# Routed rows scaled where they are made, one scatter a turn, and the shared expert's chunks moved

## The chip, the cores and the metric

The kernel runs on one core of a Trainium2 chip. The time is that of one execution on the device, in microseconds, as the median of several runs; a profiled execution gives the trace. PE (matmuls), DVE (vector), ACT (scalar), POOL (GpSimd) and SP (which issues most DMAs) are the core's engines; each works through its own list of instructions in order, and semaphores tie the lists together.

## What is computed

A decoder layer on x of 2 x 1024 tokens with 256 columns, in float32: x plus a linear attention of layernorm(x), plus a cross-attention to 154 keys with 16 heads, plus a mixture of experts. The part that the change touches is the last:

```python
scores = softmax(xf @ gate_w.T)                 # 2048 tokens, 8 experts
_, idx = top_k(scores + gate_b, 2)
w = take_along_axis(scores, idx)                # the two scores of a token
h = silu((xf @ w1[e] + b1[e]) * (xf @ w3[e] + b3[e]))      # 352 hidden
y = sum over the token's two experts e of  w_e * (h @ w2[e] + b2[e])
z = the same expert formula with the shared weights, for every token
x = x + y + z
```

The 8 experts work only on the tokens that chose them; a token's two rows are found by routing.

## The kernel before

The 2048 tokens are four blocks of 512, each of four tiles of 128 tokens. The linear attention and norms come first; the cross-attention is one software-pipelined loop of 64 turns (one turn is a tile and four heads), `for n in range(N + 6)`. In turn n, PE computes the scores of turn n+1 (L1142), DVE weighs and masks them (L1151, L1163), ACT takes the exponential (L1172), POOL divides by the sums (`divide`, s at L1180 and sr at L1183, one turn later), and PE transposes the divided rows (L1096, in `turn`) three turns later and multiplies them by the values (L1114, L1123). Steps of other work (`ahead`) are drawn into the turns from a list: the layernorm of a finished block (`finish`, with rstd on POOL at L274 and L275 and xn on DVE at L280) and its `router`.

`router` takes a block's tokens: the scores (gate matmuls L790), the two choices, and for each token and choice the slot of a row in the table `x_tab` in DRAM. A row of `x_tab` holds the normalised token (256 columns), its number and a half code: DX = 258 columns. `scatter` (POOL: a small memset L871, then an indirect DMA L872) writes the 128 rows of a tile to the slots of one choice, so there are two scatters a tile, eight a block and 32 in all. They are appended to a list, `scatters`; `put_rows()` issues all that stand in it, once a turn (in the loop right after `divide`) and between the pieces of the list behind the loop. `router` appends two at a step. The scores that the chosen slots carry are gathered in `gate` (L885, L886).

Behind the loop a list written out by hand orders the rest: the last blocks' layernorm and router (`late`), the output projections (`wo`), the pieces of the shared expert (`dense[blk]`) and the table of routed blocks (`table`). A piece of `dense` is a chunk (one of three column groups of the hidden layer, eight matmuls L935, ACT L940, DVE L943, Silu L924) or two output tiles (L955, added to x by DVE at L961, for blocks 2 and 3 followed by the store L913).

Then `routed` works through 36 blocks of 128 slots, three stages deep: `fetch` (POOL gathers rows of `x_tab`, L1427), `turn_in` (transposes L1450, ACT copy L1454), `up` (L1462, DVE L1468 and L1472), `gate_up` (ACT Silu L1476), `turn_hidden` (L1482, DVE L1486 and the target row `to`, L1488 to L1494) and `down` (L1500, ACT copy to y L1508, POOL scatter to `y_tab` L1509). The first gathers wait for the last scatter of `x_tab`. At i == n of its loop, in the drain, it draws one piece of `dense[2]`; `weigh_rows`, drawn in at i == 4, sorts each token's two scores into the order of its two rows (`by`). A further body, for more than 36 blocks, runs only if the routing needs it; with these inputs it does not.

At the end `combine` loads the two rows of every token from `y_tab` (L1543, 16 loads of 256 KB on SP's queue) and adds them to x, each times its column of `by`, with one DVE scalar_tensor_tensor (L1550) for a tile and a choice: 32 of 128x256. Its steps alternate with the last pieces of `dense[2]` and `dense[3]`.

Of the kernel before, what the change touches and what calls it, by code (L numbers as in the profile page):

```python
# [15 lines left out]
P = 128  # L16
# [9 lines left out]
def tile_decoder_layer(  # L26
# [139 lines left out]

    DX = D + 2
    x_tab = tc.dram_tile([E * REG, DX], F32, name="x_tab")  # L170
    y_tab = tc.dram_tile([2 * NTOK + P, D], F32, name="y_tab")

# [612 lines left out]
    def router(part, blk, lnT, xn, t0, nt):  # L785
# [57 lines left out]
        nc.vector.tensor_tensor(eq, ch_t, row(halves), ALU.mult)  # L843
        nc.vector.tensor_reduce(xn[:, some, D + 1], eq, AX.X, ALU.add)
        nc.gpsimd.tensor_copy(xn[:, some, D], tok2[:, ts])
        yield
        pp = mm_tile()
        nc.tensor.matmul(
# [32 lines left out]
        for t in tiles:  # L881
            for i in range(2):
                scatters.append(lambda t=t, i=i: scatter(t, i))
            if t == t0:
                nc.vector.tensor_tensor(eq2, hot[:, :, ts, :], both(sc), ALU.mult)  # L885
                nc.vector.tensor_reduce(gate[:, :, ts], eq2, AX.X, ALU.add)  # L886
            yield

    puts = []
# [6 lines left out]

    gap_t = rwp.tile([P, 1], F32, tag="gap", name="gap_t")
    NT = NTOK // P
    gate = rwp.tile([P, 2, NT], F32, tag="gate", name="gate")
    slot = rwp.tile([P, 2, NT], I32, tag="slot", name="slot")  # L900
    carry = [rwp.tile([P, E], F32, tag=f"carry{i}", name=f"carry{i}") for i in range(NBLK + 2)]

# [140 lines left out]
    with bctx:  # L1043
# [257 lines left out]
        with region:  # L1301
            for pair in range(2):
                groups[0].q_proj(pair)()
            sc[0] = score(*steps[0])
            for n in range(N + 6):
                i, t = divmod(n, TPB)
                if n + 1 < N:
                    sc[n + 1] = score(*steps[n + 1])
                if n < N:
                    s = ss[n % len(ss)]  # L1310
                    weigh(*steps[n], sc.pop(n), s)
                for take in behind:
                    take()
                behind = []
                for take in later:
                    take()
                later.clear()
                if n < N:
                    nm = hide(*steps[n], s)
                take_later()  # L1320
                if 0 <= n - 3 < N:
                    g3, t3 = steps[n - 3]
                    g3.turn(t3, ss[(n - 3) % len(ss)], srs[(n - 3) % len(srs)])

                if n + LEAD < N:
                    g4, t4 = steps[n + LEAD]
                    g4.load(t4)
                if t < 2 and i + 1 < len(groups):
                    groups[i + 1].q_proj(t)()
                if open_ and (t % 2 == 0 or open_[0][0] == NBLK - 2):  # L1330
                    blk, u = open_.pop(0)
                    behind.append(project_out(blk, u))
                    if u == TPB - 1:
                        behind.append(lambda blk=blk: side.append(finish(blk)))
                if t == 3 and 0 < i <= len(groups):
                    gv = groups[i - 1]
                    take = gv.values()
                    take(0)
                    behind.append(lambda take=take: take(1))
                    if gv.g == NG - 1:  # L1340
                        open_ += [(gv.blk, u) for u in range(TPB)]
                ahead()
                if n == N - TPB:
                    hb = ctx.enter_context(tc.tile_pool(name="hb", bufs=2, side="right"))
                    Ws_sb = shared_weights(hb)
                    dense = [
                        shared_expert(blk, hb, Ws_sb, store if blk >= 2 else None)
                        for blk in range(NBLK)
                    ]
                if N <= n < N + NHC:  # L1350
                    on(dense[0], 1)
                elif n >= N:
                    ahead()


                if n < N:
                    sums[n] = power(s, nm)
                if n - 1 in sums:
                    divide(ss[(n - 1) % len(ss)], srs[(n - 1) % len(srs)], sums.pop(n - 1))
                if n < N:  # L1360
                    put_rows()
            for take in behind:
                take()
            while side:
                ahead()

            def project_out_of(blk, u):
                project_out(blk, u)()
                yield

            turns[0] = 0
            late = [finish(NBLK - 1), finish(NBLK)]
            wo = (None for of in open_ for _ in project_out_of(*of))
            put_rows(6)
            on(wo, 1)
            on(late[0], 1)
            tabs = ctx.enter_context(tc.tile_pool(name="tabs", bufs=1, side="right"))
            table = block_table(tabs)  # L1380
            next(table)
            for which, pieces in (
                (late[0], 1), (wo, 1), (late[0], 2), (wo, 1),
                (late[0], 1), (late[1], 1), (late[0], 1), (late[1], 1), (late[0], 3),
                (dense[1], 1), (late[1], 2), (dense[1], 1), (late[1], 1), (late[0], 1),
                (late[1], 2), (late[0], 2), (late[1], 2), (dense[1], 1), (dense[0], 1),
                (late[1], 1), (late[0], 1), (late[1], 1), (table, 1), (late[1], 2),
                (dense[0], 1), (dense[1], 2), (dense[2], 1),
            ):
                on(which, pieces)  # L1390
                put_rows()
# [26 lines left out]
    class Slots:  # L1418
# [59 lines left out]
        def turn_hidden(self):  # L1478
            i = self.i
            tp = mm_tile()  # L1480
            for c in range(NHC):
# [4 lines left out]
            nc.vector.tensor_copy(self.hT.rearrange("p c q -> p (c q)"), tp[:, :HW_])  # L1486
            to_f = mpool.tile([P, 1], F32, tag="to_f", name="to_f")
            nc.vector.scalar_tensor_tensor(  # L1488
                to_f, self.xb[:, D + 1 :], eidx[:, i : i + 1], self.xb[:, D : D + 1],
                ALU.is_lt, ALU.add,  # L1490
            )
            nc.vector.tensor_tensor(to_f, to_f, beyond[:, i : i + 1], ALU.add)
            self.to = mpool.tile([P, 1], I32, tag="to", name="to")
            nc.vector.tensor_tensor(self.to, to_f, away, ALU.min)  # L1494

        def down(self):
            po = mm_tile()
# [7 lines left out]
                    start=(c == 0), stop=(c == NHC - 1),  # L1505
                )
            y = mpool.tile([P, D], F32, tag="y", name="y", bufs=2)
            nc.scalar.copy(y, po[:, :D])  # L1508
            nc.gpsimd.indirect_dma_start(  # L1509
                out=y_tab, in_=y, in_offset=None,  # L1510
                out_offset=bass.IndirectOffsetOnAxis(ap=self.to[:, 0:1], axis=0),
            )


    by = tab_tile([P, 2, NT], "by")

    def weigh_rows():
        num = tab_tile([P, 2, NT, E], "num")
        nc.vector.tensor_tensor(
            num, hot,  # L1520
            iota_f[:, :E].unsqueeze(1).unsqueeze(1).to_broadcast([P, 2, NT, E]), ALU.mult,
        )
        who = tab_tile([P, 2, NT], "who")
        nc.vector.tensor_reduce(who, num, AX.X, ALU.add)
        swap = tab_tile([P, 2, NT], "swap")
        nc.vector.tensor_tensor(swap[:, 0], who[:, 0], who[:, 1], ALU.is_gt)
        nc.vector.tensor_scalar(swap[:, 1], swap[:, 0], -1.0, 1.0, ALU.mult, ALU.add)
        other = tab_tile([P, NT], "other")
        for i in range(2):
            nc.vector.tensor_tensor(by[:, i], gate[:, 0], swap[:, 1 - i], ALU.mult)  # L1530
            nc.vector.tensor_tensor(other, gate[:, 1], swap[:, i], ALU.mult)
            nc.vector.tensor_tensor(by[:, i], by[:, i], other, ALU.add)

    def combine():

        tiles = [(blk, t) for blk in (2, 3, 0, 1) for t in range(TPB)]
        yts = {}
        for blk, t in tiles:
            at = blk * TPB + t
            yt = yts[blk, t] = W_sb[:, at // 2, (at % 2) * 2 * D : (at % 2 + 1) * 2 * D].rearrange(  # L1540
                "p (i d) -> p i d", i=2
            )
            nc.sync.dma_start(  # L1543
                out=yt,
                in_=y_tab[2 * P * at : 2 * P * (at + 1), :].rearrange("(p i) d -> p i d", i=2),
            )
        for blk, t in tiles:
            at = blk * TPB + t
            for i in range(2):
                nc.vector.scalar_tensor_tensor(  # L1550
                    xr[blk][:, t, :], yts[blk, t][:, i, :], by[:, i, at : at + 1],
                    xr[blk][:, t, :], ALU.mult, ALU.add,
                )
            if blk < 2:
                store(blk, t)
            yield

    back = combine()
# [5 lines left out]
    def routed(blocks, fill=None):  # L1564
# [7 lines left out]
        for i in range(n + 2):  # L1572
# [7 lines left out]
                blocks[i + 2].turn_in()  # L1580
            if i < n:
                blocks[i].gate_up()
            elif fill and i == n:
                next(fill)
            if i >= 2:
                blocks[i - 2].down()
            if fill and i == 4:
                weigh_rows()


    NF = NB - (E - 1) // 2
# [2 lines left out]
        skip_runtime_bounds_check_because="a sum of counts of blocks",  # L1594
    )
    with tc.manual_schedule(engines=ENGINES):
        routed([Slots(i) for i in range(NF)], dense[2])
    with tc.If(used > NF):
        with tc.manual_schedule(engines=ENGINES):
            routed([Slots(i) for i in range(NF, NB)])  # L1600
    with tc.manual_schedule(engines=ENGINES):

        for blk, some in zip((2, 3, 3, 2, 3, 2, 3, 3), (1, 3, 3, 2, 3, 2, 2, 0)):
            next(dense[blk])
            on(back, some)

# [64 lines left out]
```

## Time and profile before

| what | value |
|---|---|
| median of 3 runs | 642.95 us (641.51 to 643.62) |
| profiled execution | 642.6 us, span 640.9 us |
| mean granted TensorE clock | 0.989 |
| PE busy | 602.3 us, 94% of the span |
| DVE busy | 432.5 us, 67% |
| ACT busy | 296.7 us, 46% |
| POOL busy | 249.3 us, 39% |
| cross-attention turns of the scatters of blocks 0 and 1 | 285 to 325 us, 360 to 384 us |
| routed blocks | 453 to 604 us |
| combine | 615 to 638 us |

The span is the time from the first to the last instruction in the trace; what lies outside it is 1.7 us. A line of a trace answer gives the start, the duration, the engine, the line of the kernel, the operation, the tiles written and read with their partitions and elements, and in brackets how long the engine had been idle and what ended that. Busy shares overlap between engines; what counts is which engine the others wait for in a stretch.

### The profile page before, as it was taken

Reading aid. Unit: us, or ns where it says so; the run is one execution under the profiler, and the core shown is the slowest. Engines: PE = TensorE matmul, PEld = TensorE weight load, DVE = VectorE, ACT = ScalarE, POOL = GpSimd, SP = SyncE. Lnnn points to the kernel's source line nnn. Section 1 sums busy time; section 2 is a strip of 40 time slices with the busy share of each in tenths; the row PEclk is TensorE's granted clock in tenths of the full one; section 3 lists DMA queues with packets and bytes.
Section 4 is the critical chain, followed back from the end, with each engine's and each line's share of the span. In section 5 each row is a group of like instructions: output and inputs, shape, how many; then the busy total and the mean of one; then the engine's idle time right before and its main releaser. Section 6 shows DMA issues by size and latency. Waiting matters only on the chain.

```text
span 640.9 us, 10242 instructions
## 1 busy us (share of the span) xinstructions
PE 602.3 (94%) x3024; PEld 389.2 (61%) x3024; DVE 432.5 (67%) x1380; ACT 296.7 (46%) x895; POOL 249.3 (39%) x377
## 2 busy tenths in 40 slices
PE   4998989999999998999999979999799999999996
PEld 3553556545677445776468554766577777777654
DVE  4877995789835899556975693367365665556547
ACT  2423586777636676446884665231222222222220
POOL 4913042522315223228642581625344444444110
PEclk9999999999999999999999989999899999999999
DMA  8800579967966554245552320798112122221065
GB/s 292 241 16 6 129 185 259 216 153 175 237 158 145 145 137 104 52 125 129 119 125 65 91 75 1 222 333 301 49 59 67 58 67 63 63 67 59 33 209 203
DMA packets 111683, 83.79 MB, mean 131 GB/s; under 512 B 41874, under 2 KB 105091, under 8 KB 111500
## 3 DMA queue, kind: packets, MB, share of 16 engines
q1 hardware_dynamic: 106588, 69.42, 42.1%
q0 software_dynamic: 4992, 13.71, 6.7%
q8 instruction: 26, 0.43, 0.3%
q14 instruction: 29, 0.24, 0.1%
q10 hardware_dynamic: 48, 0.00, 0.0%
HBM read 54.90 MB, written 27.98 MB: 129 GB/s over the span
## 4 chain that ended last, share of the span: by engine, by line
PE 64%; DVE 15%; POOL 6%; issue 4%; ACT 4%; DMA 3%; SPq 2%; DVEq 0%; POOLq 0%; ACTq 0%
PE sc L1462 14%; PE mm L1193 8%; PE mm L1500 6%; PE sc L935 5%; PE mm L1076 4%; PE mm L586 3%; PE sc L1142 3%; PE tp L1096 3%; DVE s L1163 3%; PE mm L1114 3%; POOL x_tab L872 3%; DVE rks L521 2%; DVE s L1151 2%; PE mm L494 2%; PE tp L1500 2%
## 5 line engine op out<-in xcount | busy, mean ns | idle before, releaser
L1180 POOL TENSOR_TENSOR s<-s,sums 128x512 f32<-128x512 f32 x64 | 66.8, 1044 | 179.6 <-DVE sums L1179 167.1
L1172 ACT ACTIVATE s<-s,nm 128x154 f32<-128x154 f32 x256 | 104.8, 417 | 5.7 <-DVE nm L1163 5.7
L1462 PE MATMUL sc<-W_sb,xT 128*128 x288 | 92.8, 466 | 0.2 <-issue 0.2
L1163 DVE CUSTOM_DVE_ANT_0 s<-s,mk 128x154 f32<-128x154 f32 x256 | 90.7, 408 | 1.2
L1509 POOL DMA_INDIRECT y_tab<-y,to x36 | 35.5, 985 | 83.6 <-DVE to_f L1488 57.4
L1462 PEld LDWEIGHTS sc<-W_sb,xT 128*128 128x128 f32 x288 | 52.8, 193 | 24.0 <-issue 1.7
L1468 DVE TENSOR_TENSOR ea<-sc,b 128x704 f32<-128x704 f32 x36 | 32.1, 892 | 51.9 <-PE sc L1462 51.8
L1076 PE MATMUL mm<-lnT,Wq_sb 128*128 128x512 f32 x128 | 61.6, 604 | 2.6 <-DVE k L516 2.0
L1097 ACT COPY pT<-tp 128x512 f32<-128x512 f32 x64 | 36.9, 576 | 45.1 <-PE tp L1096 44.8
L1193 PE MATMUL mm<-Wo_sb,oT 128*128 128x256 f32 x256 | 57.6, 379 | 0.0
L1142 PEld LDWEIGHTS sc<-kT,qT 64*128 64x128 f32 x512 | 36.5, 186 | 29.0 <-issue 10.9
L1142 PE MATMUL sc<-kT,qT 64*128 64x154 f32 x512 | 50.5, 316 | 3.5 <-DVE s L1151 2.8
L1193 PEld LDWEIGHTS mm<-Wo_sb,oT 128*128 128x128 f32 x256 | 48.0, 190 | 8.8 <-issue 2.4
L1151 DVE TENSOR_TENSOR s<-sc,fs 128x616 f32<-128x616 f32 x64 | 49.9, 780 | 0.9 <-PE sc L1142 0.9
L1096 PE MATMUL tp<-ident,s 128*128 128x128 f32 x256 | 42.7, 290 | 8.0 <-POOL s L1180 7.5
L1172 ACT ACTIVATION_READ_ACCUMULATOR s<-s,nm 128x1 f32 x256 | 49.6, 194 | 0.0
L935 PE MATMUL sc<-lnT,Ws_sb 128*128 128x512 f32 (+1 forms) x96 | 43.1, 595 | 0.8 <-ACT y L1508 0.4
L494 PE MATMUL mm<-lnT,wqkv_sb 128*128 128x512 f32 x88 | 41.4, 600 | 0.7 <-DVE lnT L225 0.4
L1500 PE MATMUL mm<-W_sb,hT 128*128 x168 | 41.1, 380 | 0.7 <-DVE to_f L1488 0.7
L1427 POOL DMA_INDIRECT xb<-x_tab,rows_i x36 | 34.7, 965 | 16.3 <-issue 9.4
L1096 PEld LDWEIGHTS tp<-ident,s 128*128 128x128 f32 x256 | 27.8, 144 | 20.1 <-issue 9.6
L872 POOL DMA_INDIRECT x_tab<-xn,slot x32 | 32.9, 1029 | 14.6 <-DVE req L885 9.6
(245 smaller groups left out, 1024.3 us busy)
## 6 DMA issues: line engine op xcount, KB each, us to landing
fs<-in_fside SPq DMA_DIRECT2D x64, 308.0 KB
x_tab<-book SPq DMA_DIRECT2D x32, 516.0 KB
W_sb<-in_w SPq DMA_DIRECT2D x16, 352.0 KB
mk<-in_mask SPq DMA_DIRECT2D x64, 77.0 KB
W_sb<-y_tab SPq DMA_DIRECT2D x16, 256.0 KB
b<-b_tab SPq DMA_DIRECT2D x1, 2816.0 KB
W_sb<-in_w SPq DMA_DIRECT2D x8, 256.0 KB
out<-xr SPq DMA_DIRECT2D x16, 128.0 KB
```

Of the source, the lines that this page charges most:

```text
L494: nc.tensor.matmul(ps, lhsT=wqkv_sb[:, c, o * P : (o + 1) * P], rhs=lnTa[self.blk][:, c, :], start=(c == 0), stop=(c == ND - 1),)
L935: nc.tensor.matmul(ps[:hn, :], lhsT=Ws_sb[:, at : at + hn], rhs=lnT[:, d, :], start=(d == 0), stop=(d == ND - 1),)
L1076: nc.tensor.matmul(ps, lhsT=Wq_sb[:, c, o * P : (o + 1) * P], rhs=lnTq[self.blk][:, c, :], start=(c == 0), stop=(c == ND - 1),)
L1096: nc.tensor.transpose(tp[:, j * P : (j + 1) * P], s[:, j, :P], ident)
L1142: nc.tensor.matmul(sc[:, par, pair * SK : (pair + 1) * SK], lhsT=gr.qT[pair][rows, t * P : (t + 1) * P], rhs=kT[rows, 2 * gr.g + pair, gr. ...
L1151: begun = nc.vector.tensor_tensor(s[:, :, :SK].rearrange("p (pair par) k -> p par pair k", par=2), sc[:, :, : 2 * SK].rearrange("p par (pa ...
L1163: nc.vector.tensor_tensor_reduce(s[:, j, :], s[:, j, :], gr.mk[t][:, j, :], MASKED, FLOOR, ALU.add, ALU.min, nm[:, j : j + 1],)
L1172: nc.scalar.activation(s[:, j, :SK], s[:, j, :SK], AF.Exp, bias=nm[:, j : j + 1], scale=-1.0, accum_out=sums[:, j : j + 1],)
L1180: nc.gpsimd.tensor_tensor(s[:, :, :P], s[:, :, :P], sums.unsqueeze(2).to_broadcast([P, HG, P]), ALU.mult)
L1193: nc.tensor.matmul(ps[:, :D], lhsT=oTs[blk][o][:, t * P : (t + 1) * P], rhs=Wo_sb[0][:, o, :], start=(o == 0), stop=(o == NO - 1),)
L1462: nc.tensor.matmul(ab[:, j, :HID], lhsT=self.xT[:, d, :], rhs=W_sb[:, bass.ds(ev, 1), at : at + HID].rearrange("p a h -> p (a h)"), start= ...
L1500: nc.tensor.matmul(po[:, :D], lhsT=self.hT[:kn, c, :], rhs=W_sb[:kn, bass.ds(self.ev, 1), O2 + c * D : O2 + (c + 1) * D].rearrange("p a d ...
```

## The change

Six edits:

1. A row of `x_tab` grows by eight columns and carries the token's eight scores (a POOL copy in `router`). The score gathers for `gate`, and `weigh_rows`, go.
2. In `turn_hidden` DVE copies the score of the block's expert out of the row (`by`, 128x1, at a register offset), and in `down` ACT scales y by it instead of copying.
3. `combine` then adds without a factor, and takes two tiles at once: 16 tensor_tensor of 128x512 instead of 32 of 128x256. The loads and stores are the same ones.
4. In the loop `put_rows(1)`: one scatter a turn.
5. Two chunks of `dense[2]` instead of one stand at the end of the list ahead of the gathers.
6. In the drain a piece is drawn at i == n and at i == n + 1 (the last chunk of `dense[2]`, the first of `dense[3]`); after it two chunks and eight output tiles are left instead of four and eight.

```diff
@@ -166,7 +166,7 @@
 
 
 
-    DX = D + 2
+    DX = D + 2 + E
     x_tab = tc.dram_tile([E * REG, DX], F32, name="x_tab")
     y_tab = tc.dram_tile([2 * NTOK + P, D], F32, name="y_tab")
 
@@ -843,6 +843,7 @@
         nc.vector.tensor_tensor(eq, ch_t, row(halves), ALU.mult)
         nc.vector.tensor_reduce(xn[:, some, D + 1], eq, AX.X, ALU.add)
         nc.gpsimd.tensor_copy(xn[:, some, D], tok2[:, ts])
+        nc.gpsimd.tensor_copy(xn[:, some, D + 2 :], sc)
         yield
         pp = mm_tile()
         nc.tensor.matmul(
@@ -881,9 +882,6 @@
         for t in tiles:
             for i in range(2):
                 scatters.append(lambda t=t, i=i: scatter(t, i))
-            if t == t0:
-                nc.vector.tensor_tensor(eq2, hot[:, :, ts, :], both(sc), ALU.mult)
-                nc.vector.tensor_reduce(gate[:, :, ts], eq2, AX.X, ALU.add)
             yield
 
     puts = []
@@ -896,7 +894,6 @@
 
     gap_t = rwp.tile([P, 1], F32, tag="gap", name="gap_t")
     NT = NTOK // P
-    gate = rwp.tile([P, 2, NT], F32, tag="gate", name="gate")
     slot = rwp.tile([P, 2, NT], I32, tag="slot", name="slot")
     carry = [rwp.tile([P, E], F32, tag=f"carry{i}", name=f"carry{i}") for i in range(NBLK + 2)]
 
@@ -1358,7 +1355,7 @@
                 if n - 1 in sums:
                     divide(ss[(n - 1) % len(ss)], srs[(n - 1) % len(srs)], sums.pop(n - 1))
                 if n < N:
-                    put_rows()
+                    put_rows(1)
             for take in behind:
                 take()
             while side:
@@ -1385,7 +1382,7 @@
                 (dense[1], 1), (late[1], 2), (dense[1], 1), (late[1], 1), (late[0], 1),
                 (late[1], 2), (late[0], 2), (late[1], 2), (dense[1], 1), (dense[0], 1),
                 (late[1], 1), (late[0], 1), (late[1], 1), (table, 1), (late[1], 2),
-                (dense[0], 1), (dense[1], 2), (dense[2], 1),
+                (dense[0], 1), (dense[1], 2), (dense[2], 2),
             ):
                 on(which, pieces)
                 put_rows()
@@ -1486,12 +1483,14 @@
             nc.vector.tensor_copy(self.hT.rearrange("p c q -> p (c q)"), tp[:, :HW_])
             to_f = mpool.tile([P, 1], F32, tag="to_f", name="to_f")
             nc.vector.scalar_tensor_tensor(
-                to_f, self.xb[:, D + 1 :], eidx[:, i : i + 1], self.xb[:, D : D + 1],
+                to_f, self.xb[:, D + 1 : D + 2], eidx[:, i : i + 1], self.xb[:, D : D + 1],
                 ALU.is_lt, ALU.add,
             )
             nc.vector.tensor_tensor(to_f, to_f, beyond[:, i : i + 1], ALU.add)
             self.to = mpool.tile([P, 1], I32, tag="to", name="to")
             nc.vector.tensor_tensor(self.to, to_f, away, ALU.min)
+            self.by = mpool.tile([P, 1], F32, tag="by", name="by")
+            nc.vector.tensor_copy(self.by, self.xb[:, D + 2 :][:, bass.ds(self.ev, 1)])
 
         def down(self):
             po = mm_tile()
@@ -1505,54 +1504,33 @@
                     start=(c == 0), stop=(c == NHC - 1),
                 )
             y = mpool.tile([P, D], F32, tag="y", name="y", bufs=2)
-            nc.scalar.copy(y, po[:, :D])
+            nc.scalar.activation(y, po[:, :D], AF.Copy, scale=self.by[:, 0:1])
             nc.gpsimd.indirect_dma_start(
                 out=y_tab, in_=y, in_offset=None,
                 out_offset=bass.IndirectOffsetOnAxis(ap=self.to[:, 0:1], axis=0),
             )
 
 
-    by = tab_tile([P, 2, NT], "by")
-
-    def weigh_rows():
-        num = tab_tile([P, 2, NT, E], "num")
-        nc.vector.tensor_tensor(
-            num, hot,
-            iota_f[:, :E].unsqueeze(1).unsqueeze(1).to_broadcast([P, 2, NT, E]), ALU.mult,
-        )
-        who = tab_tile([P, 2, NT], "who")
-        nc.vector.tensor_reduce(who, num, AX.X, ALU.add)
-        swap = tab_tile([P, 2, NT], "swap")
-        nc.vector.tensor_tensor(swap[:, 0], who[:, 0], who[:, 1], ALU.is_gt)
-        nc.vector.tensor_scalar(swap[:, 1], swap[:, 0], -1.0, 1.0, ALU.mult, ALU.add)
-        other = tab_tile([P, NT], "other")
-        for i in range(2):
-            nc.vector.tensor_tensor(by[:, i], gate[:, 0], swap[:, 1 - i], ALU.mult)
-            nc.vector.tensor_tensor(other, gate[:, 1], swap[:, i], ALU.mult)
-            nc.vector.tensor_tensor(by[:, i], by[:, i], other, ALU.add)
-
     def combine():
 
-        tiles = [(blk, t) for blk in (2, 3, 0, 1) for t in range(TPB)]
+        pairs = [(blk, a) for blk in (2, 3, 0, 1) for a in range(TPB // 2)]
         yts = {}
-        for blk, t in tiles:
-            at = blk * TPB + t
-            yt = yts[blk, t] = W_sb[:, at // 2, (at % 2) * 2 * D : (at % 2 + 1) * 2 * D].rearrange(
-                "p (i d) -> p i d", i=2
-            )
-            nc.sync.dma_start(
-                out=yt,
-                in_=y_tab[2 * P * at : 2 * P * (at + 1), :].rearrange("(p i) d -> p i d", i=2),
-            )
-        for blk, t in tiles:
-            at = blk * TPB + t
+        for blk, a in pairs:
+            row = W_sb[:, blk * 2 + a, : 4 * D].rearrange("p (b i d) -> p b i d", b=2, i=2)
+            yts[blk, a] = row
+            for b in range(2):
+                at = blk * TPB + 2 * a + b
+                nc.sync.dma_start(
+                    out=row[:, b],
+                    in_=y_tab[2 * P * at : 2 * P * (at + 1), :].rearrange("(p i) d -> p i d", i=2),
+                )
+        for blk, a in pairs:
+            dst = xr[blk][:, 2 * a : 2 * a + 2, :]
             for i in range(2):
-                nc.vector.scalar_tensor_tensor(
-                    xr[blk][:, t, :], yts[blk, t][:, i, :], by[:, i, at : at + 1],
-                    xr[blk][:, t, :], ALU.mult, ALU.add,
-                )
+                nc.vector.tensor_tensor(dst, yts[blk, a][:, :, i, :], dst, ALU.add)
             if blk < 2:
-                store(blk, t)
+                for b in range(2):
+                    store(blk, 2 * a + b)
             yield
 
     back = combine()
@@ -1580,12 +1558,10 @@
                 blocks[i + 2].turn_in()
             if i < n:
                 blocks[i].gate_up()
-            elif fill and i == n:
-                next(fill)
+            elif fill:
+                next(fill[i - n])
             if i >= 2:
                 blocks[i - 2].down()
-            if fill and i == 4:
-                weigh_rows()
 
 
     NF = NB - (E - 1) // 2
@@ -1594,13 +1570,13 @@
         skip_runtime_bounds_check_because="a sum of counts of blocks",
     )
     with tc.manual_schedule(engines=ENGINES):
-        routed([Slots(i) for i in range(NF)], dense[2])
+        routed([Slots(i) for i in range(NF)], dense[2:])
     with tc.If(used > NF):
         with tc.manual_schedule(engines=ENGINES):
             routed([Slots(i) for i in range(NF, NB)])
     with tc.manual_schedule(engines=ENGINES):
 
-        for blk, some in zip((2, 3, 3, 2, 3, 2, 3, 3), (1, 3, 3, 2, 3, 2, 2, 0)):
+        for blk, some in zip((3, 2, 3, 2, 3, 3), (1, 1, 2, 1, 2, 1)):
             next(dense[blk])
             on(back, some)
```

## The prediction

> **What bounds the kernel now.** I read the page first, for the busy shares by slice.
>
> ```profile
> PE 602.3 (94%) x3024; PEld 389.2 (61%) x3024; DVE 432.5 (67%) x1380; ACT 296.7 (46%) x895; POOL 249.3 (39%) x377
> ...
> PE   4998989999999998999999979999799999999996
> ...
> PEclk9999999999999999999999989999899999999999
> ```
>
> PE is the bound: 38.6 us of the 640.9 us span is all that PE is not busy, and two dents (the digit 7, slices 24 and 29) are no start or end effect. The clock row has a dent beside each. So a gain has to come out of PE's waits, PE's slow clock, or the tail after PE's last matmul. The waits of PE name the first:
>
> ```profile
> PE tp L1096 <- POOL s L1180: 7.5, 5, 2.3
> ...
> PE tp L1450 <- DMA xb<-x_tab,rows_i: 3.3, 1, 3.3
> ```
>
> The first line is transposes that wait for POOL's division; by windows, 5.4 of the 7.5 lie in 340 to 392 us and 1.0 in 285 to 325, the two places where scatters run inside the turns. The second line is the first gathered rows (the second gather adds 0.8). The timeline of POOL in a scatter turn:
>
> ```profile
> 373.84 1.05 POOL L1180 TENSOR_TENSOR s<-s,sums 128x512 f32<-128x512 f32 x1
> 374.83 0.45 POOL L1183 TENSOR_TENSOR sr<-s,sums 128x104 f32<-128x104 f32 x1
> ...
> 375.48 1.11 POOL L872 DMA_INDIRECT x_tab<-xn,slot  x1 [0.15 <-issue]
> ...
> 377.94 1.05 POOL L1180 TENSOR_TENSOR s<-s,sums 128x512 f32<-128x512 f32 x1
> ```
>
> A turn is 1.44 us of division and two scatters of 1.3 us each (memset 0.1, gap 0.2, issue 1.0): 4.10 us from s to s. PE needs about 2.56 a turn (24 us less its 5.4 of waits and about 0.7 of slow clock, for 7 turns). After the waits, a slow clock; the windows of 1 us (PE, PEld, DVE, ACT, POOL busy, then the granted clock):
>
> ```profile
> 381.00:382.00 1.00, 1.00 (x6) 1.00 (x6) 0.96 (x4) 1.00 (x7) 1.00 (x2) 0.50 0.00 0
> ...
> 454.00:455.00 1.00, 1.00 (x3) 0.67 (x2) 0.00 (x0) 0.00 (x0) 0.74 (x1) 0.50 0.34 95
> ```
>
> It stands at 0.50 from 380.9 to 387.7 and from 452.3 to 456. The timeline across the gather gap, and of the first combine:
>
> ```profile
> 443.89 3.70 PE L935 MATMUL sc<-lnT,Ws_sb 128*128 128x512 f32 x8 [0.38 <-DVE xr L961]
> ...
> 450.86 0.41 PE L1450 MATMUL tp<-ident,xb 128*128 128x128 f32 x2 [3.27 <-DMA xb<-x_tab,rows_i]
> ...
> 452.70 3.62 PE L1462 MATMUL sc<-W_sb,xT 128*128 x6 [0.21 <-issue]
> ...
> 617.91 1.01 DVE L1550 SCALAR_TENSOR_TENSOR xr<-W_sb,by,xr 128x256 f32<-128x256 f32 x2 [1.74 <-DMA W_sb<-y_tab]
> ```
>
> From 453 to 604 PE is busy in every window, 4.07 us a block. From 617.91 to 637.5 DVE is without a pause, the last store is issued at 637.8 and the span ends at 640.9: there DVE is the bound. The sum below is made against the profiled execution (642.6 us, 1.7 outside its span); the median, 642.95, is 0.35 above it.
>
> **A. One scatter a turn.** The eight scatters of block 1 go over turns 56 to 63 instead of 56 to 59; POOL's turn falls from 4.1 to 2.74, against PE's 2.56. Counted on POOL alone, the divisions for turns 56, 58 and 59, for which PE waited 1.15, 1.95 and 2.29, come 1, 3 and 4 scatters earlier: 1.3, 3.9 and 5.2 us, enough for all 5.4 us. But DVE was full from 363 to 383 as well, 5.4 us of it in operations that stand while POOL divides: one L1163 took 3.00 us instead of 0.31 across two divisions that ran back to back, two L280 2.27 instead of 0.8. A scatter between divisions breaks up the first (2.7); the others collide as before. So 0 to 5.4 is regained; I take half, **2.7**. If more is regained, ACT's exponentials, which wait for DVE, are late next.
>
> Clock: in the slow spell L790 took 2.61 against 1.95 at 242 us, and with L1096, L1114 (3.68 against 1.94) and L1123 it cost about **3.4**. It followed idles of 1.95 and 2.29 us, five microseconds apart. An idle of 0.97 at 310 us brought none; idles of 1.17 and 1.24 at 246 and 252 did (0.50 at 254 to 258). With residual waits near 1 us it can go either way; I take it as gone.
>
> The Trainium skill (page "TensorE: Matmul & The Clock Gate", Part 1, on the clock gate) says the clock is halved after about one idle window of some 3.4 us, the window running free. By that rule no idle here, 2.29 at most, halves it; the trace does not agree, with 0.50 after a pair of idles that sum to 4.2, so the rows decide.
>
> Block 0's scatters are spread likewise; PE waited 0.97 there once: **0.9**.
>
> **B. A second chunk ahead of the gathers.** The chunk of 3.44 us (8 matmuls) follows the one that ends at 447.59 and ends at 451.05. The rows arrive at 450.86 and 452.08 whatever PE does, since their gathers wait for the last scatter's landing; so the chunk lies in the 3.27 us wait and delays the first transposes by 0.2. Expert 0's matmuls start at 452.70 as before. What is won is the clock: six of them took 3.62, and all eight 4.21 against 2.37 at full clock, 1.84. POOL has five more copies of about 0.2 us (as COPY xn<-tok), two of them ahead of the last scatters: 0.3 lost. **1.5**, from 0 to 1.8. If this cover failed (rows there already at 447.6), the chunk would cost 3.44 here; nothing in the landing times says so. ACT's eviction of the chunk (0.69) stands ahead of the first xT copy (451.31 to 451.75), which still ends before the second, the one that up waits for.
>
> **C. Drain and tail.** At 606.51, T, the drain's first chunk ends in both kernels. Now one more chunk (dense[3], 3.44) stands between the hidden transposes and the last down, into an idle of 0.74: the last y is about 2.5 later, 613.2, its scatter 613.85 instead of 611.94 (before, that scatter also waited for the one ahead to land). SP's loads, queued behind it, 617.0 instead of 615.09; the first add waits for two of them (0.54 each), so 620.4 instead of 617.91. Then DVE has 16 adds of 128x512. The trace has this form as L540 and L533 at 0.68, a pitch of 0.66: 10.6, against 14.6 for the 32 L1550 at a pitch of 0.455. With eight L961 (0.33) and one or two L943 (0.67) the list is about 14 us, and DVE ends near 634.6 instead of 637.53. The loads' own pace allows it: 16 in 12.7 us before, so the last pair lands about 630. PE's last output is near 631, no bound. The final pair's two stores cost 0.34 more than one. **2.5**; from 0 (loads pace the adds) to 3.5.
>
> **At nothing.** Each block gets a DVE copy of 128x1 (with a register instruction; its like, L1494, 0.16 to 0.21) and y is scaled on ACT instead of copied (0.36; the nearest row with an ACTIVATE, L1476 over 352 columns, takes 0.50, so up to 0.14 more). Per block DVE has 2.56 and ACT 1.22 busy of PE's 4.07; hs is ready 3.3 us before its use. weigh_rows (ten small DVE operations) and the gate's two per router part go: they lay beside PE, nothing won. Rows of the table grow from 258 to 266 columns: 3% on 32 clearing writes and the gathers, beside DMA shares of 0.6 to 0.8.
>
> **Sum.** 2.7 + 3.4 + 0.9 + 1.5 + 2.5 = 11.0: 642.6 - 11.0 = 631.6, as a median 632.0.
>
> **Rivals.**
> 1. The clock stays slow near 380, or a residual wait starts a new spell later: 3.4 less is won, 635.4. For it: idles near 1.2 us sufficed once, POOL's 2.74 is over PE's 2.56. Against it: 0.97 did not.
> 2. The tail gives nothing: the loads, 1.9 later, meet stores and land slower than the adds need. DMA share there is 1.0 for 12 us, which speaks for it; 14 us of DVE work after the first pair's landing against 10 for the other seven pairs speaks against. 634.5; with rival 1 together 637.9.
> 3. Slower: the routed stage's block becomes longer. The scale column is read by a register offset on DVE and then by ACT, whose y frees the buffer that down needs; if ACT had to change its function table between Silu and the scaled copy, two loads of 1.283 us (the row ACT_TABLE_LOAD) a block would give ACT 1.22 + 2.57 = 3.8 of 4.07, with hops between engines over it. It decides from 4.07 + 0.31 (11.0 over 36 blocks); at 4.5 a block, 0.45 x 36 = 16 is lost, 648. Against it: the order of instructions shows no more table loads than before.
> 4. It does not do what it says: scatters still bunch, the dense chunk in the gap finds its rows or buffer late. Only the tail and a part of the clock is left, about 3: 640, within the bound.
>
> The Trainium skill's page "GPSIMD Engine Reference" (Key points) says that GpSimd shares SBUF interfaces with VectorE, which contend where DVE reads two SBUF inputs; L1163's 3.00 us agrees. By that rule alone, with all of DVE's 5.4 us kept, part A's 2.7 would be zero: 634.7.
>
> **How the numbers follow.** Forecast 0.50, rival 1 0.20, rival 2 (alone or with 1) 0.15, rival 3 0.07, rival 4 0.08. A measurement of this kernel can tell about 0.3%, 1.9 us, from no change: faster is under 641.0, slower over 644.9. Faster takes the forecast, rivals 1 and 2 and some of 4, 0.88; same, most of rival 4, 0.05; slower, rival 3, 0.07. Low end: all 5.4 of the stall and 1.0 more of the tail, about 628.3, less a small margin; high end: rivals 1 and 2 together, 637.9, and a half: 627.5 to 638.5.
>
> **What would show it.** In the changed profile: the wait of L1096's transposes for POOL falls from 7.5 to about 3 or less; no clock of 0.50 near 375 to 385, nor at the first block; the wait for xb falls from 3.3 to under 0.5, with two chunks ahead of it; blocks stay at 4.07; 16 TENSOR_TENSOR 128x512 at 0.68 in the tail, DVE full from the first to the last, the first about 14 us after the drain's chunk ends. It is wrong if the blocks lengthen, if POOL's waits come back in turns 60 to 63, or if DVE waits for loads in the tail.

## The result, and the profile after

The changed kernel takes 635.92 us (median of 4 runs, 635.34 to 637.0) against 643.16 for the kernel before: ratio 0.9895, 95% interval 0.9866 to 0.9924. Timed again later (run e9 below) it took 633.57 us against 641.87, ratio 0.9861 (0.9833 to 0.9889). So it is faster by 7 to 9 us; 11 were forecast. The first profiled execution took 635.73 us with a span of 634.0, 6.86 us less than the span before.

The page, for the busy shares and the clock by slice:

```profile
PE 600.5 (95%) x3024; PEld 388.0 (61%) x3024; DVE 426.4 (67%) x1380; ACT 299.7 (47%) x895; POOL 249.2 (39%) x382
...
PE   4998999999999998999999989999999999999994
...
PEclk9999899999999999799999999999999999999998
```

Of PE's two dents one is gone (slice 29) and one is an 8 (slice 24). The clock row has lost its dents in those slices, as forecast. But it has two others, in slices 5 and 17, in a stretch that the change doesn't touch: slow spells, stretches at a granted clock of 0.50, from 63.7 and from 254.8 us. The waits of PE:

```profile
PE tp L1093 <- ACT pT L1094: 2.6, 4, 1.3
...
PE tp L1093 <- POOL s L1177: 1.1, 1, 1.1
...
PE mm L1447 <- DMA xb<-x_tab,rows_i: 0.8, 1, 0.8
...
PE tp L1093 <- POOL gap_t L872: 0.5, 1, 0.5
...
PE tp L1447 <- DMA xb<-x_tab,rows_i: 0.3, 1, 0.3
```

The transposes (L1093 now, L1096 before) wait 1.1 us for POOL's division instead of 7.5, and the first rows are waited for 0.3 instead of 3.3. New is the first line: 2.6 us for ACT's copy of the transposed rows. POOL in a turn with a scatter, by its timeline:

```profile
375.88 1.03 POOL L1177 TENSOR_TENSOR s<-s,sums 128x512 f32<-128x512 f32 x1
376.88 0.43 POOL L1180 TENSOR_TENSOR sr<-s,sums 128x104 f32<-128x104 f32 x1
...
377.50 1.11 POOL L873 DMA_INDIRECT x_tab<-xn,slot  x1 [0.15 <-issue]
378.64 1.05 POOL L1177 TENSOR_TENSOR s<-s,sums 128x512 f32<-128x512 f32 x1
```

From s to s it is 2.76 us; 2.74 was forecast, 4.10 was before. The gather gap, on the timeline of all engines:

```profile
439.02 7.13 PE L932 MATMUL sc<-lnT,Ws_sb 128*128 128x512 f32 x16
...
446.46 0.41 PE L1447 MATMUL tp<-ident,xb 128*128 128x128 f32 x2 [0.31 <-DMA xb<-x_tab,rows_i]
...
448.39 2.60 PE L1459 MATMUL sc<-W_sb,xT 128*128 x8 [0.28 <-issue]
```

Two chunks in one row (16 matmuls), then 0.31 us of idle, and the first block's eight matmuls take 2.60 us. And the beginning and the end of the tail:

```profile
610.79 9.76 SPq L1523 DMA_DIRECT2D W_sb<-y_tab  x16
...
616.28 1.42 DVE L1530 TENSOR_TENSOR xr<-W_sb,xr 128x512 f32<-128x512 f32 x2 [3.50 <-DMA W_sb<-y_tab]
...
629.08 1.41 DVE L1530 TENSOR_TENSOR xr<-W_sb,xr 128x512 f32<-128x512 f32 x2
```

The first add comes 5.49 us after the first load is issued (2.82 before), with DVE idle for 3.50 us of that.

Where the time went, by the time at which the same instruction starts in the two traces:

| from and to | before | after | gain |
|---|---|---|---|
| start to the transposes of turn 36 (unchanged stretch) | 279.76 | 282.93 | -3.17 |
| to turn 50 (scatters of block 0) | 58.32 | 57.57 | 0.75 |
| turn 55 to turn 63 (scatters of block 1) | 32.31 | 25.45 | 6.86 |
| turn 63 to the first block's matmuls | 56.49 | 56.62 | -0.13 |
| to T, where PE starts what follows the drain's first chunk | 153.81 | 151.98 | 1.83 |
| T to the end of the span | 34.38 | 33.66 | 0.72 |

Between turns 50 and 55 nothing changes. So the parts gained 10.0 us together, and 3.2 were lost ahead of all of them.

### The profile page after: what moved, and what is told of

It reads as the page before. It is cut to its first block, busy times and chain, and to the rows that moved or that the text cites. A ratio compares the mean times of both kernels' runs of the same rounds, so it can differ in the third digit from the quotient of the medians.

```text
span 634.0 us, 10283 instructions
## 1 busy us (share of the span) xinstructions
PE 600.5 (95%) x3024; PEld 388.0 (61%) x3024; DVE 426.4 (67%) x1380; ACT 299.7 (47%) x895; POOL 249.2 (39%) x382
## 4 chain that ended last, share of the span: by engine, by line
PE 63%; DVE 14%; DMA 7%; ACT 7%; issue 4%; SPq 2%; POOL 2%; DVEq 0%; POOLq 0%; ACTq 0%
PE sc L1459 13%; PE mm L1190 8%; PE mm L1499 5%; PE mm L1073 5%; PE sc L1139 4%; PE tp L1093 3%; PE mm L586 3%; ACT s L1169 3%; PE mm L1111 3%; DVE s L1160 3%; PE sc L932 3%; PE mm L494 3%; DMA y_tab<-y,to 2%; PE mm L1120 2%; PE tp L1499 2%
## 5 line engine op out<-in xcount | busy, mean ns | idle before, releaser
L1160 DVE CUSTOM_DVE_ANT_0 s<-s,mk 128x154 f32<-128x154 f32 x256 | 92.2, 413 | 1.2
L1459 PE MATMUL sc<-W_sb,xT 128*128 x288 | 91.2, 460 | 0.3 <-issue 0.3
L1073 PE MATMUL mm<-lnT,Wq_sb 128*128 128x512 f32 x128 | 63.8, 623 | 2.5 <-DVE k L516 2.0
L1093 PE MATMUL tp<-ident,s 128*128 128x128 f32 x256 | 42.1, 288 | 4.2 <-ACT pT L1094 2.6
L1093 PEld LDWEIGHTS tp<-ident,s 128*128 128x128 f32 x256 | 27.3, 142 | 16.2 <-issue 11.1
```

The lines of the kernel that those rows point to most:

```text
L1073: nc.tensor.matmul(ps, lhsT=Wq_sb[:, c, o * P : (o + 1) * P], rhs=lnTq[self.blk][:, c, :], start=(c == 0), stop=(c == ND - 1),)
L1093: nc.tensor.transpose(tp[:, j * P : (j + 1) * P], s[:, j, :P], ident)
L1160: nc.vector.tensor_tensor_reduce(s[:, j, :], s[:, j, :], gr.mk[t][:, j, :], MASKED, FLOOR, ALU.add, ALU.min, nm[:, j : j + 1],)
L1459: nc.tensor.matmul(ab[:, j, :HID], lhsT=self.xT[:, d, :], rhs=W_sb[:, bass.ds(ev, 1), at : at + HID].rearrange("p a h -> p (a h)"), start= ...
```

## The experiments

Four kernels isolate parts, one repeats the change, one joins two parts, and four (one of them two edits together) look into the tail. All were timed against runs of the kernel before on the same chip.

**One scatter a turn alone.**

```diff
-                    put_rows()
+                    put_rows(1)
```

> The kernel before with one scatter a turn, and nothing else of the change. Theory 1 (each part does its own work, the clock's slow spells fall by chance of phase): the wait of the transposes for POOL, 7.5 us before, falls to 1 to 2, the spell of 0.50 near 380 us is gone, and turn 63 comes 5 to 7 us earlier against the point where the turns of the scatters begin; the time falls by 4 to 6.5 us, to 636.5 to 639, less 1.7 for each slow spell more that the profile shows ahead of 285 us. Rival (the turns are bound by DVE and POOL together, so what POOL's wait loses another wait takes): the turns gain under 2.5 us and the time is over 640.5. On the spells ahead of 285 us: if the wider rows and their copies bring them, this kernel, which has none, shows before's (one at 254 us, 3.4 us long); if they are chance, it may show others.

Measured: 636.02 us against 642.21, ratio 0.9902 (0.9878 to 0.9926), 6 us of the change's 7 to 9. Waits of PE:

```profile
PE tp L1096 <- ACT pT L1097: 2.6, 4, 1.3
PE tp L1096 <- POOL s L1180: 1.1, 1, 1.1
```

Turn 55 to turn 63 takes 25.44 us, 6.87 less than before, and no window between 360 and 400 has a clock under 1.00. Theory 1 holds, a little above its figures; the rival, under 2.5 us, falls. This kernel has the slow spell at 64 us, though its rows are as narrow as before: the wider rows don't bring it.

**All waiting scatters again, the rest kept.**

```diff
-                    put_rows(1)
+                    put_rows()
```

> The changed kernel with all waiting scatters issued in a turn again (two a turn in four turns); the rest of the change is kept. Theory 1: it loses what one scatter a turn brought, 4 to 6.5 us: about 640 to 642, with the transposes' wait for POOL near 5 us in the last turns and a slow spell there. Rival (little of the change's gain comes from the scatters): under 638.

Measured: 641.36 us, ratio 0.9973 (0.9952 to 0.9995), inside theory 1's 640 to 642: what is left without the scatters is about 2 us. In windows of 1 us its clock:

```profile
377.00:378.00 1.00, 1.00 (x6) 0.78 (x4) 0.99 (x4) 0.59 (x1) 0.97 (x2) 0.50 0.00 0
382.00:383.00 1.00, 1.00 (x7) 1.00 (x6) 0.96 (x2) 0.73 (x3) 1.00 (x2) 0.50 0.00 0
388.00:389.00 1.00, 1.00 (x6) 0.24 (x2) 0.00 (x0) 0.00 (x0) 0.12 (x1) 0.50 0.00 0
```

It has the division waits back (1.15, 1.95 and 0.81 in the three turns) and a slow spell twice as long as before's, 13.65 us from 375.8. Over all profiles the spell near 380 stands in all four with two scatters a turn (before, e2, e3, e7) and in none of the eight with one.

**The second chunk alone.**

```diff
-                (dense[0], 1), (dense[1], 2), (dense[2], 1),
+                (dense[0], 1), (dense[1], 2), (dense[2], 2),
...
-        for blk, some in zip((2, 3, 3, 2, 3, 2, 3, 3), (1, 3, 3, 2, 3, 2, 2, 0)):
+        for blk, some in zip((3, 3, 2, 3, 2, 3, 3), (1, 3, 3, 3, 2, 2, 2)):
```

> The kernel before with a second chunk of dense[2] ahead of the gathers (in the tail three chunks and eight output tiles are left, and combine is as before). Theory 1: the first rows are waited for 0.3 us instead of 3.3, the first block's eight matmuls take 2.6 instead of 4.2 us, so the drain begins 1.5 to 1.8 us earlier; in the tail DVE is the bound and has one L943 of 0.67 us less: the time falls by 1.5 to 2.5, to about 641. Rival (the chunk is paid for at the gathers and nothing returns): the time is within 1 us of before.

Measured: 641.51 us, ratio 0.9978 (0.9962 to 0.9994). PE's timeline:

```profile
445.53 7.13 PE L935 MATMUL sc<-lnT,Ws_sb 128*128 128x512 f32 x16 [0.37 <-DVE xr L961]
453.39 0.41 PE L1450 MATMUL tp<-ident,xb 128*128 128x128 f32 x2 [0.72 <-DMA xb<-x_tab,rows_i]
...
455.34 2.60 PE L1462 MATMUL sc<-W_sb,xT 128*128 x8 [0.28 <-issue]
```

The wait is 0.72 instead of 3.27 and the first matmuls are at full clock. In this profile the rows came 0.97 us later than before's (the gathers began 4.88 us after the chunks did, 4.03 before), so less than half of the 1.7 was kept. From the first block's matmuls to the second's it is 2.66 us in all nine profiles with the second chunk, and 4.26 to 4.35 in the three without it (before, e1, e3): 1.6 to 1.7 is gained there each time, and the landing of the last scatter takes from it or adds to it by up to 1.2 us. From turn 63 to the end of the span this profile takes as long as before's (0.24 us less to T, 0.24 more behind it), so its tail with one chunk less was not shorter, and the time, 0.7 us under before's, meets the rival's mark: the clock's gain is real, but the later rows took most of it here.

**The scaled rows alone.** The changed kernel with the lines of e7 and of e2 put back, `dense[2]` alone in the drain, and four chunks and eight output tiles behind it:

```diff
-        for blk, some in zip((3, 2, 3, 2, 3, 3), (1, 1, 2, 1, 2, 1)):
+        for blk, some in zip((2, 3, 3, 2, 3, 2, 3, 3), (0, 1, 2, 1, 1, 1, 1, 1)):
```

> The changed kernel without one scatter a turn and without the moved chunks: rows with scores, y scaled by ACT, sixteen adds over two tiles, four chunks and eight output tiles in the tail as before. Theory 1: blocks of 4.07 us as before, the tail's DVE work 4.0 us less but its start up to 1 us later, since the first add waits for two loads; the time falls by 2 to 3.5, to about 640. Rival (an instruction fetch or the sharing of the DMA engines makes the second load late, whatever the order): the first add starts over 4.5 us after the first load is issued and the gain is under 1.5. Spells ahead of 285 us: if the wider rows bring them, this kernel shows the changed kernel's (one at 63 to 67 us and 6.8 us from 255).

Measured: 643.1 us, ratio 1.0006 (0.9987 to 1.0025): nothing, where 2 to 3.5 us were expected. The first add comes 3.65 us after the first load, so the rival's late second load is not the reason here. DVE's timeline shows what is:

```profile
621.77 0.75 DVE L940 SCALAR_TENSOR_TENSOR a<-sc,b_sb,a 128x512 f32<-128x512 f32 x1 [1.09 <-ACT a L937]
...
627.79 0.75 DVE L940 SCALAR_TENSOR_TENSOR a<-sc,b_sb,a 96x512 f32<-96x512 f32 x1 [0.39 <-ACT a L937]
...
634.81 0.42 DVE L958 TENSOR_TENSOR xr<-tp,xr 128x256 f32<-128x256 f32 x1 [0.51 <-PE tp L952]
```

DVE now waits for work that comes out of PE, the last time for the last output tile: with four chunks in the tail PE ends at 634.8 and bounds it. Of the four microseconds less of DVE work, 2.0 went into these waits and 1.9 into a later first add (T + 13.3 instead of T + 11.4). The edit to combine needs the moved chunks.

**The change once more.** The same kernel.

> The changed kernel once more, for another profile and a narrower interval. Theory (slow spells by chance of the clock's phase): the slow spells ahead of 285 us stand elsewhere or are of another length than in the first profile (63.7 for 3.4 us, 254.8 for 6.8), while the stretches that the change touches keep their gains to 0.3 us: turn 55 to turn 63 takes 25.4 to 25.6 us, the first add comes 5.2 to 5.5 us after the first load is issued. Rival (the change brings the spells): the same spells again. Median 635 to 636.5.

Measured: 633.57 us, ratio 0.9861 (0.9833 to 0.9889), lower than the 635 to 636.5 expected. No spell at 64 us in this profile, one of 6.83 us from 253.5; turn 55 to turn 63 takes 25.45 us, and the first add comes 5.04 after the first load, just under the 5.2 expected:

```profile
64.00:65.00 1.00, 1.00 (x3) 0.20 (x2) 1.00 (x2) 0.00 (x0) 0.00 (x0) 1.00 0.00 0
258.00:259.00 1.00, 1.00 (x3) 0.38 (x2) 0.11 (x1) 0.00 (x0) 1.00 (x4) 0.50 0.00 0
```

The same program has the spell at 64 in one execution and not in the other: chance, not the change.

**The drain without dense[3].**

```diff
-        routed([Slots(i) for i in range(NF)], dense[2:])
+        routed([Slots(i) for i in range(NF)], dense[2:3])
...
-            elif fill:
-                next(fill[i - n])
+            elif fill and i == n:
+                next(fill[0])
...
-        for blk, some in zip((3, 2, 3, 2, 3, 3), (1, 1, 2, 1, 2, 1)):
+        for blk, some in zip((3, 3, 2, 3, 2, 3, 3), (0, 1, 1, 2, 1, 2, 1)):
```

> The changed kernel with dense[3]'s first chunk back behind the drain, so that the last down does not wait for it; combine's adds over two tiles stay. Theory 1 (the late first add is one part of the second load, held up by an instruction fetch that falls into it; PE's place in its list sets when that is): here the loads are issued some 2.5 us earlier against the drain, the fetch falls later than the first two loads, and the first add comes 3.4 to 3.7 us after the first load is issued. Rival (the second of sixteen loads is always that late): 5 us or more. The time: the adds start about 4 us earlier against the drain's first chunk, but PE then has the chunk in the tail and ends 3.4 us later against it, near 30 us; the list of adds can gain no more than PE's end allows, so the time is within 1 us of the changed kernel.

Measured: 632.56 us, ratio 0.9842 (0.9812 to 0.9871), not told apart from the change's by the intervals. The first add comes 3.56 us after the first load, as theory 1 had it; the rival's 5 us falls. Two of the expectation's figures were wrong: the loads are issued only 0.4 us earlier against T (the last but one y waits on ACT for the gate of the drain's chunk, which stayed, and the last scatter, issued at 605.53 though its y is done at 603.23, stands behind the landing of the one ahead, at 604.79), and PE's end was no bound. From T to the end of the span it takes 32.7 us, 1.0 less than in the change's first profile and 0.5 less than in its second; the chunk moved into the drain bought nothing that its later loads did not cost.

**The output tiles ahead of the first adds.**

```diff
-        for blk, some in zip((3, 2, 3, 2, 3, 3), (1, 1, 2, 1, 2, 1)):
+        for blk, some in zip((3, 2, 3, 2, 3, 3), (0, 2, 2, 1, 2, 1)):
```

The stores of two tiles of block 2 are thereby put ahead of the adds of their routed rows, which those stores leave out.

> The changed kernel with the first pair of adds behind the first two output tiles' adds on DVE (PE's list is the same). Theory 1 (DVE is idle 3.5 us ahead of the first pair, and its 14 us of list is the bound from there): the two L958 of 0.75 us together go into the idle time, the tail ends 0.7 us earlier: ratio to the changed kernel 0.999. Rival (another wait, for PE or loads, follows at once): no change.

Measured: 637.98 us, ratio 0.9925 (0.9897 to 0.9954), slower than the change. DVE's timeline:

```profile
621.15 2.75 DVE L1530 TENSOR_TENSOR xr<-W_sb,xr 128x512 f32<-128x512 f32 x4 [6.98 <-DMA W_sb<-y_tab]
```

The first adds stand 7 us, though the second load has landed at 615.7: they must not overwrite the two tiles before the stores have read them. On SP the two stores are issued between the loads, the first behind seven of them, the second behind one more:

```profile
615.07 0.37 SPq L910 DMA_DIRECT2D out<-xr  x1
...
616.02 0.38 SPq L910 DMA_DIRECT2D out<-xr  x1
```

They land at 619.85 and 620.85, and the adds follow at 621.15. The experiment was badly chosen and says nothing on its question.

**Two parts without the scaled rows.** The edits of e1 and e2 together.

> The kernel before with one scatter a turn and the second chunk ahead of the gathers, but without rows that carry scores: 32 scalar_tensor_tensor in combine. Theory 1 (the parts add up: e1 gave 6.3, e2 1.4, the scaled rows alone nothing): 642.2 - 7.7 = 634.5, as fast as the changed kernel or a little faster. Rival (the scaled rows gain their 2 us only together with the moved chunks): over 636.5.

Measured: 633.66 us, ratio 0.9876 (0.9848 to 0.9903). Within the intervals this is as fast as the whole change (its six runs go from 633.08 to 635.97, those of the change beside them from 631.93 to 634.7), and the rival, over 636.5, falls: rows with scores, y scaled on ACT, the wide adds and the chunk in the drain add nothing that can be measured. From T to the end its profile takes 33.66 us, as the change's first.

**Adds one tile at a time.**

```diff
-                nc.vector.tensor_tensor(dst, yts[blk, a][:, :, i, :], dst, ALU.add)
+                nc.vector.tensor_tensor(
+                    xr[blk][:, t, :], yts[blk, t][:, i, :], xr[blk][:, t, :], ALU.add
+                )
```

> The changed kernel with combine's unscaled adds one tile at a time: 32 tensor_tensor of 128x256 instead of 16 of 128x512. Theory 1 (the first add is late because it needs the second load, one part of which an instruction fetch holds up by about 2 us; and a 128x256 add has a pitch of 0.33, half of the 0.66 of the wide one, so that pairing saves nothing): the first add comes 3.3 to 3.5 us after the first load is issued instead of 5.0 to 5.5, the adds of the first tile go ahead in that time, and the list is as long as before: the time falls by 0.5 to 0.8 against the changed kernel. Rival (two tiles at once save DVE time): the adds take over 11.5 us together and the time rises.

Measured: 633.31 us, ratio 0.9878 (0.9847 to 0.9909), no difference from the change. The first add comes 2.94 us after the first load, but the second tile's waits again; groups on DVE, this kernel and then the changed one:

```profile
L1530 DVE TENSOR_TENSOR xr<-W_sb,xr 128x256 f32<-128x256 f32 x32 | 12.8, 422 | 2.7 <-DMA W_sb<-y_tab 2.2
```

```profile
L1530 DVE TENSOR_TENSOR xr<-W_sb,xr 128x512 f32<-128x512 f32 x16 | 10.8, 687 | 3.8 <-DMA W_sb<-y_tab 3.5
```

32 narrow adds take 2.0 us more than 16 wide ones: the pitch is 0.40, not 0.33 as taken from L961 (L958 here). Two rows of this kernel's DVE timeline show where the difference lies:

```profile
614.20 0.75 DVE L958 TENSOR_TENSOR xr<-mm,xr 128x256 f32<-128x256 f32 x2
...
623.20 3.27 DVE L1530 TENSOR_TENSOR xr<-W_sb,xr 128x256 f32<-128x256 f32 x8
```

The two L958 add to two different tiles and start 0.33 us apart. The eight L1530 are two adds to each of four tiles: by the trace's starts it is 0.45 us from the first add of a tile to the second, which waits for DVE's own semaphore, and 0.34 to the first add of the next tile, which does not. So it is the second add's wait for the first one that costs, and not that both operands are in SBUF. What the earlier start won, the longer list lost; theory 1 was half wrong.

**Both.** The edits of e4 and e12 together.

> Both: dense[3]'s first chunk behind the drain and the unscaled adds one tile at a time. Theory 1: loads issued earlier, first add 2.8 us after the first load as in the kernel before, no wait for a second load; 0.5 to 1 us under the kernel with the chunk moved alone (ratio to before 0.9842): 0.983, about 631.5. Rival (PE's end or the loads' pace bounds the tail already): the same 0.984.

Measured: 633.24 us, ratio 0.9876 (0.9848 to 0.9903). No better; the 629.7 us span of its profile had neither the spell at 64 us nor any near 380 or 450. None of the variants is shown to beat the changed kernel.

## Why the prediction was right, and where it missed

The direction, the largest part (A) and the mechanisms of A and B were right; C, from which the second most was expected, gave least. The forecast of 632.0 lies 3.9 below the first median and 1.6 below the second, both inside the range. The parts came to 10.0 of the 11.0, and 3.2 were lost where no step looked. Step by step:

- **A, scatters of block 1.** Forecast 6.1, measured 6.86. Of it 3.47 are waits of PE (0.20, 1.15, 1.95 and 2.29 before; 0.54, 1.26 and 0.32 after), and the rest, 3.4, is what the prediction gave the clock. The stall was put at 2.7, half of the 5.4, and came out at 3.5. The reason given, that a scatter between divisions breaks up DVE's longest blocked operation, fits: no L1160 there takes over 1.24 us, against 3.00. What is late next is ACT's copy of the transposes, which stands behind four exponentials in ACT's list.
- **The clock near 380** went, as taken, in all eight profiles with one scatter a turn; this was the step held most open (rival 1). The residual idle of 1.26 us did not slow it.
- **A', block 0.** Forecast 0.9, measured 0.75.
- **B.** Forecast 1.5, measured 1.83 less 0.13 (1.0 in e9). That the chunk lies inside the wait for rows was right; how late the rows are varies, from turn 63 to the first block's matmuls it is 55.28 to 57.46 us in the nine profiles with the second chunk.
- **C, the mis-sized term.** Forecast 2.5, measured 0.72 (1.2 in e9). The wide adds have a pitch of 0.66 as taken, the list from the first to the last add is 14.2 us (14 forecast), the loads are issued at T + 10.42 (10.5). The step that failed is the landing of the second load, put one issue behind the first: the first add came at T + 15.9 and not at T + 13.9. The prediction named a DVE that waits for loads in the tail as a sign of being wrong, and here it does, for 3.50 us; behind the first add it waits for none, so the loads' pace (rival 2) was not the reason. By the trace's landing records 15 of the second load's 16 parts are there at 614.11 and the last at 616.19. A 16 KB packet of a queue of the kind "instruction" starts at 613.65:

```profile
q8 instruction: 1, 0.02, 1.2%
```

  In the five profiles (after, e5, e7, e9, e12) in which this packet starts 2.4 to 2.9 us after the first load's issue, the second load's last part is 1.4 to 2.1 us behind the others; in the seven in which it starts 4.2 us after or later, 0.4 at most. Before, it came 9.9 us after, when DVE was behind the loads anyhow, and cost nothing. In all twelve profiles the packet starts when 41 to 46 matmuls are left in PE's list, so when it falls in the tail depends on how many matmuls were moved out of it. That a packet of 0.96 us holds one part back by two is a coincidence in time shown seven against five (and forecast once, for e4), not a cause that was tested alone.
- **C, the whole.** Even without that the term is worth nothing by itself: e3, with the wide adds alone, gained nothing since PE bounds the tail, and e10, with the other parts and no wide adds, is as fast as all together. With the cheaper adds DVE bounds the tail only once PE's chunks are out of it. So of the six edits the one scatter a turn and the second chunk carry all of the gain that can be measured.
- **What no step held.** 3.17 us were lost ahead of turn 36: a slow spell of 3.41 us at 63.7, behind an idle of 1.97 us for k that the kernel before has too, and one of 6.83 instead of 3.41 at 254.8. The windows, after and then before:

```profile
64.00:65.00 1.00, 1.00 (x2) 0.34 (x1) 1.00 (x2) 0.00 (x0) 0.00 (x0) 0.50 0.00 0
258.00:259.00 1.00, 1.00 (x5) 0.96 (x5) 0.90 (x8) 0.13 (x1) 0.00 (x0) 0.50 0.04 14
```

```profile
64.00:65.00 1.00, 1.00 (x4) 0.38 (x2) 1.00 (x2) 0.00 (x0) 0.00 (x0) 1.00 0.00 0
258.00:259.00 1.00, 1.00 (x4) 0.49 (x4) 0.27 (x1) 0.11 (x1) 1.00 (x3) 1.00 0.01 1
```

  The wider rows do not bring them: the spell at 64 us stands in e1, e2 and e10, whose rows are as narrow as before's, and not in e3, e9 and e11, whose rows are wide. The transposes of turn 36 start at 279.4 to 279.8 us in the three profiles that have neither the spell at 64 nor a long one near 255 (before, e3, e11), at 280.6 to 281.8 in the eight with one of the two, and at 282.9 in the one with both, the change's first. So the 11.0 was forecast against a profiled execution that had neither.
- **Routed stage.** The slower rival did not come. The blocks' matmuls start 4.22 us apart before and after; the 4.07 of the prediction is the 146.4 us from the first block's matmuls to the last's over 36, and not the pitch. y takes 0.46 us scaled and 0.36 copied, the column's copy 0.15, both hidden as taken.
- **A reading.** The waits of 1.95 and 2.29 us near 380, which the prediction puts five microseconds apart, end 4.1 us apart; nothing in the sum hangs on it.

## What to carry to other kernels

Where an engine off the critical path delivers a bit too late in a few turns, spreading its bursts evenly can win twice: the waits go, and the clock does not fall behind them. Taking work off the engine that bounds a tail is worth what the next bound allows, so look for PE's end and the first load's landing before costing it. A saving of a few microseconds is forecast better as a sum over stretches than as a total, since slow spells in untouched stretches move the total by 3 us.

## What the runs showed of the hardware

- The slow spells come in whole multiples of 3.41 us (3.41, 6.83, 13.65 by the trace's clock record), at a granted clock of 0.50, and those of one execution start on one grid of that step (before: 254.57, 380.86 and 452.54, 37 and 21 steps apart). An idle of 1.97 us that ends at 63.3 to 64.4, in all twelve profiles, starts one at 64 us in eight and not in four, in two executions of one program with both outcomes.
- Which it is goes with where the 3.41 us grid lies: in the eight with the spell the whole idle falls into one step of the grid, in the four without a step's edge cuts it, and 1.86 us at most lie in one step. The Trainium skill (page "TensorE: Matmul & The Clock Gate", Part 1) has the free-running window of 3413 ns, and the trace agrees on its length and on its running free; that an idle must fill a window does not hold here, with 1.97 us enough in some positions. The idle in one step is not all that counts: near 255 us 1.24 us of it are followed by a spell in all twelve profiles, near 375 us 1.60 are not (before, e3).
- DVE's adds of 128x256 start 0.33 to 0.34 us apart when they go to different tiles, with one operand in PSUM or with both in SBUF, and 0.45 when the second adds to the tile that the first wrote; at 128x512 it is 0.61 and 0.72. A pitch taken from a row of independent operations is too short for a chain of dependent ones.
